# A new order for all engines in a state-space layer, half a product more on GpSimd, and the input image added earlier

## The chip, the cores and the metric

The kernel runs on one core of a Trainium2 chip. The metric is the device time of one execution in microseconds (us), as the median of the runs. The engines are TensorE (PE in the profile, PEld for its weight loads), VectorE (DVE), ScalarE (ACT), GpSimd (POOL) and the DMA queues, of which SyncE (SP) feeds the one used for plain transfers and GpSimd the one used for scatters.

## The reference, cut to what matters

Two layers on 32 images of 128 channels and 56 x 56 pixels, in float32. Layer 0 is a convolution with a mixture of experts, layer 1 a convolution with a selective scan (Mamba). With `L = 56 * 56` the tokens of an image and `DI = 256`, `DS = 16`:

```python
# layer 0: conv, LayerNorm, top 2 of 8 experts with capacity, then
return input + x_skip + layer_scale * moe_out
# layer 1, per image, t runs over the 3136 tokens
dt = softplus(dt @ dt_proj_w.T + dt_proj_b)
dA = exp(dt[..., None] * A)                      # 16 decays for each of 256 rows
dBu = dt[..., None] * Bm[:, :, None, :] * xm[..., None]
h = dA_t * h + dBu_t                             # the scan
y = einsum('bds,bs->bd', h, C_t) + xm * D
y = (y * silu(z)) @ out_proj_w.T
```

What is added at the end of layer 0 (`input + x_skip + moe_out`) is what layer 1 reads.

## The kernel before

The work runs in four stages, one after the other.

1. Layer 0's convolution, LayerNorm and routing. The normed rows go to `res_d` in DRAM, one row of 128 floats per token, each half row of 56 pixels in reversed order.
2. Dispatch: 56 batches, each of which loads 14 x 128 rows (`xg0`, six buffers deep), copies them on ScalarE (`xg1`) and scatters both with 28 indirect DMAs of GpSimd (L859) into `buf_d`. Half way, the weights of layer 1 are prepared.
3. The experts: rows are loaded from `buf_d`, go through two matrix products, and are added to `res_d` by indirect DMAs of GpSimd (L911).
4. Layer 1. Each image is cut into 7 groups of 448 tokens, 224 groups in all. A group has 16 units, one for each state. The 256 rows lie on 128 partitions as two halves.

In layer 1 the order on all engines is written out: `PLAN` lists the steps of a group, `UNITS` those of each unit, each with a place counted in units; the list of all groups is sorted by place and recorded in that order, under `manual_schedule`. Each engine then works through its own list in order and waits for semaphores. The places are an order and not times.

For a group, `fetch` loads a piece `x1` of the image and the rows `yg` of `res_d`; `moe_pe` (L1026, L1028) adds them on PE, with a permutation that turns the rows round; `moe_act` copies the sum to SBUF. Then follow a 1x1 convolution (`cv1_pe`, `cv1_act` with its tile `xh`), the variance (`sq_act`, `var_pe`, `rstd_act`, and `rstd_dve` in three tiny steps, L1090, L1092, L1095, the last of which writes `r`), `bc_pe` and `te_dve`, the projections `z_pe` and `xm_pe`, SiLU between two loads of activation tables (L1152, L1175), `px_pe`, `dt_pe`, the softplus (`sp_*`; `sp_pe` sums it into `p_sp`), and `sp_act`, which writes `dt` (L1240). `du_pool` multiplies dt and xm on GpSimd (L1245). The small matmuls share two PSUM buffers, `mm`.

For a unit: `bc_load` brings broadcast rows of B (`bb`) and C (`cb`), two units at a time. `db_pool` multiplies du and B for two units at once on GpSimd (L1336). `exp_act` writes the decays of both halves into one of two PSUM tiles, `da0` or `da1`, by the unit's parity (L1354). `scan_dve` runs the scan on VectorE (L1373, whole; L1377, by halves). `cmul` multiplies the states by C (L1397). `carry_act` saves the last state for the next group (L1405), `sum_pe` adds the product to the sum in PSUM (L1286). At the end come `yz_dve`, `out_pe` and `out_act`. rstd's first two steps work in the first four columns of da0, which the decays don't use.

`MODE` has a letter for each unit. D: whole scan in place, product on VectorE. P: whole scan into a tile `hs`, product on GpSimd. Q: as P, with the scan in two halves. M: two half scans, the first product half on VectorE, the second on GpSimd. Before it is `DQDDQDPPDDDDPDDP`: ten products on VectorE, six on GpSimd. `hs` has two buffers.

Of the kernel before, what the change touches and what calls it, by code (L numbers as in the profile page):

```python
# [42 lines left out]
MODE = 'DQDDQDPPDDDDPDDP'  # L43
PRODS = 6
PLAN = (
    (-41.157, "fetch"),
    (-34.382, "moe_pe"),
    (-32.986, "moe_act"),
    (-28.346, "cv1_pe", "p_cvc", "cv1c"),
    (-27.384, "sq_act"),  # L50
    (-26.393, "cv1_pe", "p_cv1", "cv1t"),
    (-25.274, "cv1_act"),
    (-23.306, "var_pe"),
    (-23.291, "rstd_act"),
    (-23.185, "edges_act"),
    (-20.935, "rstd_dve", 0),
    (-20.876, "rstd_dve", 1),
    (-19.458, "rstd_dve", 2),
    (-19.126, "bc_pe"),
    (-18.367, "te_dve"),  # L60
    (-18.165, "te_act"),
    (-17.77, "z_pe", 0),
    (-16.927, "z_copy", 0),
    (-15.982, "z_pe", 1),
    (-15.86, "xm_pe", 0),
    (-15.811, "xm_pe", 1),
    (-14.784, "z_copy", 1),
    (-14.441, "z_silu"),
    (-14.388, "xm_act", 0),
    (-14.349, "xm_act", 1),  # L70
    (-13.504, "tables"),
    (-13.487, "px_pe"),
    (-11.507, "px_act"),
    (-11.215, "dt_pe", 0),
    (-10.684, "dt_pe", 1),
    (-10.326, "sp_abs", 0),
    (-9.043, "sp_abs", 1),
    (-8.458, "sp_exp"),
    (-7.656, "sp_one"),
    (-6.228, "sp_w"),  # L80
    (-5.252, "sp_pe", ("w", "e", "m")),
    (-5.135, "sp_ln"),
    (-5.019, "sp_pe", ("u",)),
    (-4.678, "lt_pe", range(0, 9)),
    (-4.117, "sp_act", 0),
    (-3.918, "sp_act", 1),
    (-3.032, "lt_act", 0),
    (-3.001, "du_pool"),
    (-2.343, "lt_act", 1),
    (2.033, "lt_silu"),  # L90
    (3.656, "dd_pe"),
    (18.599, "yz_dve", 0),
    (18.857, "yz_dve", 1),
    (23.328, "out_pe"),
    (25.003, "out_act"),
# [3 lines left out]
        (-5.892, "bc_load", "bb"),  # L99
        (-3.501, "bc_load", "cb"),  # L100
        (-2.818, "db_pool"),
        (-0.991, "exp_act"),
        (-0.076, "scan_dve"),
        (0.16, "cmul", 0),
        (1.245, "carry_act"),
        (3.662, "sum_pe"),
    ),
    (
        (-2.505, "db_pool"),
        (-0.83, "exp_act"),  # L110
        (-0.619, "scan_dve"),
        (1.229, "cmul", 0),
        (3.088, "carry_act"),
        (9.441, "sum_pe"),
    ),
    (
        (-11.504, "bc_load", "bb"),
        (-2.533, "bc_load", "cb"),
        (-2.288, "db_pool"),
        (-0.633, "exp_act"),  # L120
        (-0.074, "scan_dve"),
        (0.16, "cmul", 0),
        (1.407, "carry_act"),
        (3.828, "sum_pe"),
    ),
    (
        (-3.007, "db_pool"),
        (-1.559, "exp_act"),
        (-0.609, "scan_dve"),
        (-0.338, "carry_act"),  # L130
        (0.16, "cmul", 0),
        (2.009, "sum_pe"),
    ),
    (
        (-4.093, "bc_load", "bb"),
        (-3.639, "db_pool"),
        (-0.666, "bc_load", "cb"),
        (-0.482, "exp_act"),
        (0.865, "scan_dve"),
        (1.06, "cmul", 0),  # L140
        (1.786, "sum_pe"),
        (2.033, "carry_act"),
    ),
    (
        (-4.025, "db_pool"),
        (-1.052, "exp_act"),
        (-0.068, "scan_dve"),
        (0.16, "cmul", 0),
        (1.263, "carry_act"),
        (3.791, "sum_pe"),  # L150
    ),
    (
        (-5.791, "bc_load", "bb"),
        (-4.743, "db_pool"),
        (-2.416, "bc_load", "cb"),
        (-0.463, "exp_act"),
        (0.538, "scan_dve"),
        (0.678, "cmul", 0),
        (1.758, "carry_act"),
        (4.239, "sum_pe"),  # L160
    ),
    (
        (-5.64, "db_pool"),
        (-0.299, "exp_act"),
        (-0.211, "scan_dve"),
        (1.06, "cmul", 0),
        (5.047, "sum_pe"),
        (5.187, "carry_act"),
    ),
    (  # L170
        (-7.178, "bc_load", "bb"),
        (-4.153, "db_pool"),
        (-3.514, "bc_load", "cb"),
        (-1.218, "exp_act"),
        (-0.956, "scan_dve"),
        (0.16, "cmul", 0),
        (0.466, "carry_act"),
        (0.815, "sum_pe"),
    ),
    (  # L180
        (-4.714, "db_pool"),
        (-1.825, "exp_act"),
        (-0.406, "scan_dve"),
        (0.16, "cmul", 0),
        (0.742, "carry_act"),
        (1.653, "sum_pe"),
    ),
    (
        (-8.23, "bc_load", "bb"),
        (-5.573, "bc_load", "cb"),  # L190
        (-4.053, "db_pool"),
        (-1.1, "exp_act"),
        (-0.6, "scan_dve"),
        (0.16, "cmul", 0),
        (0.996, "carry_act"),
        (1.077, "sum_pe"),
    ),
    (
        (-3.777, "db_pool"),
        (-0.685, "exp_act"),  # L200
        (-0.409, "scan_dve"),
        (0.16, "cmul", 0),
        (1.104, "sum_pe"),
        (1.278, "carry_act"),
    ),
    (
        (-7.87, "bc_load", "bb"),
        (-4.884, "bc_load", "cb"),
        (-4.31, "db_pool"),
        (-0.985, "exp_act"),  # L210
        (-0.749, "scan_dve"),
        (1.06, "cmul", 0),
        (5.159, "sum_pe"),
        (5.275, "carry_act"),
    ),
    (
        (-4.947, "db_pool"),
        (-0.443, "exp_act"),
        (0.085, "scan_dve"),
        (0.16, "cmul", 0),  # L220
        (0.197, "sum_pe"),
        (0.205, "carry_act"),
    ),
    (
        (-19.062, "bc_load", "bb"),
        (-4.926, "db_pool"),
        (-2.209, "bc_load", "cb"),
        (-1.206, "exp_act"),
        (-0.658, "scan_dve"),
        (0.16, "cmul", 0),  # L230
        (0.202, "sum_pe"),
        (0.903, "carry_act"),
    ),
    (
        (-3.892, "db_pool"),
        (-0.158, "exp_act"),
        (0.91, "scan_dve"),
        (1.06, "cmul", 0),
        (2.205, "carry_act"),
        (2.818, "sum_pe"),  # L240
# [4 lines left out]
def tile_kernel(tc: tile.TileContext, a: dict, out: bass.AP):  # L245
# [14 lines left out]
    with (  # L260
# [6 lines left out]
        res_d = dram.tile([T, C], F32, name="res_d")  # L267

        ident = const.tile([128, 128], F32, name="ident")
        make_identity(nc, ident)  # L270
        mean_w = const.tile([128, 128], F32, name="mean_w")
# [403 lines left out]
        def weights(wp, wt, pw):  # L675
# [86 lines left out]
            nc.tensor.matmul(p[:, 0:1], lhsT=mean_w, rhs=cv1b, start=True, stop=True)  # L762
# [66 lines left out]
        def apart(i, group):  # L829
            inst = i.ins  # L830
            tc.declare_no_dep(inst, group=group, reason="the rows differ")
            tc.add_to_no_dep_group(group, inst)

        with (
            tc.tile_pool(name="w3t", bufs=1, reuse_waits="tile") as w3t,
            tc.tile_pool(name="p3t", bufs=2, space=PSUM) as p3t,
            tc.tile_pool(name="dispc", bufs=1, reuse_waits="tile") as dc,
            tc.tile_pool(name="disp", bufs=6, reuse_waits="tile") as dp,
        ):
            backs = []  # L840
            for k in range(2):
                bi = dc.tile([128, QB, TT], I32, name=f"bi{k}")
                nc.gpsimd.iota(bi, pattern=[[TT, QB], [1, TT]], base=0, channel_multiplier=PT)
                backs.append(bi)
# [621 lines left out]
```

## Time and profile before

| what | value |
|---|---|
| median of 10 runs | 15843.36 us (15840.01 to 15850.96) |
| the profiled execution | 15844.33 us, its span 15842.5 us |
| mean granted clock of TensorE | 0.913 |
| busy: PE, DVE, ACT, POOL | 81%, 70%, 66%, 84% of the span |
| scatters of the dispatch (L859) | 1568, mean 1051 ns, 1767.9 to 3933.1 us |
| first and last `yg` load of layer 1 | 5878.4 and 15677.2 us |

The shares of the span are means over stages with different limits; a stage is read from a stretch of its own. A row of a group of instructions gives the line, engine, operation, tiles, shapes and count, then the total busy time and the mean duration in ns, then the idle time just before them and what ended it. A row of the order in time gives start, duration, engine, line and operation. Matmuls are pipelined and their ends are modelled, so a busy PE isn't PE at its peak.

### The profile page before, as it was taken

How to read it: one execution, taken by the hardware profiler on the slowest of the kernel's cores; microseconds unless marked ns; L12 is line 12 of the kernel's file. 1: busy time of each engine (PE TensorE's matmuls, PEld its weight loads, DVE VectorE, ACT ScalarE, POOL GpSimd, SP SyncE). 2: the span in 40 equal slices, each digit the busy share in tenths (PEclk: the TensorE clock that was granted, in tenths of full speed). 3: DMA queues.
4: the chain of work that ended last, by engine and by line, in shares of the span. 5: the costliest groups of instructions: out<-in, count | busy, mean ns of one | idle time of the engine just before them, and what ended most of it. 6: DMA issues, size and time to landing. Idle time of an engine off the chain costs nothing. (4 is left out here: it accounts for less than half of the span.)

```text
span 15842.5 us, 247520 instructions
## 1 busy us (share of the span) xinstructions
PE 12825.1 (81%) x92981; PEld 7167.8 (45%) x92981; DVE 11118.5 (70%) x11366; ACT 10517.5 (66%) x21038; POOL 13335.3 (84%) x6330
## 2 busy tenths in 40 slices
PE   7996200000999999999999999999999999999998
PEld 7996100000777764444444444444444444444444
DVE  2655400000111119999999999999999999999999
ACT  4565200000444448888888888888888888888888
POOL 2443477777888879999999999999999999999999
PEclk9997555555999999999999999999999999999999
DMA  8785422222555545555555555555555555555555
GB/s 268 230 238 175 169 72 71 71 71 65 68 72 70 72 64 184 185 184 185 185 184 185 184 185 184 185 185 184 183 183 184 185 184 183 185 183 184 183 183 171
DMA packets 1325280, 2520.85 MB, mean 159 GB/s; under 512 B 139352, under 2 KB 777136, under 8 KB 1316400
## 3 DMA queue, kind: packets, MB, share of 16 engines
q1 hardware_dynamic: 1127600, 2310.57, 45.4%
q0 software_dynamic: 196480, 194.45, 7.0%
q8 instruction: 732, 11.99, 0.3%
q14 instruction: 468, 3.83, 0.1%
HBM read 2129.06 MB, written 375.43 MB: 158 GB/s over the span
## 5 line engine op out<-in xcount | busy, mean ns | idle before, releaser
L1336 POOL TENSOR_TENSOR db<-du,bb 128x1792 f32<-128x1792 f32 x1792 | 6582.9, 3685 | 0.1
L1354 ACT ACTIVATE da<-dt,aneg 128x449 f32<-128x449 f32 x7168 | 4550.1, 639 | 372.7 <-DVE r L1095 112.0
L1373 DVE TENSOR_TENSOR_SCAN da<-da,db 128x898 f32<-128x898 f32 x2240 | 4524.3, 2020 | 0.6 <-issue 0.5
L1286 PE MATMUL py<-prod,ident 64*64 64x448 f32 x28672 | 3223.5, 547 | 117.6 <-DVE prod L1397 111.1
L1397 POOL TENSOR_TENSOR prod<-hs,cb 128x896 f32<-128x896 f32 x1344 | 2608.4, 1941 | 217.9 <-issue 157.1
L1397 DVE TENSOR_TENSOR prod<-da,cb 128x896 f32<-128x896 f32 x2240 | 2440.1, 1089 | 133.4 <-DMA cb<-bc_d 14.9
L859 POOL DMA_INDIRECT buf_d<-xg,slot x1568 | 1647.4, 1051 | 522.6 <-issue 518.3
L911 POOL DMA_INDIRECT res_d<-ys,xb x984 | 1591.8, 1618 | 350.8 <-issue 281.9
L951 PE MATMUL ept<-ident,xb 128*128 128x128 f32 (+1 forms) x984 | 189.0, 274 | 2078.9 <-DMA xb<-buf_d 2078.6
L1373 DVE TENSOR_TENSOR_SCAN hs<-da,db 128x898 f32<-128x898 f32 x896 | 1786.1, 2014 | 0.1
L1286 PEld LDWEIGHTS py<-prod,ident 64*64 64x64 f32 x28672 | 1008.8, 132 | 1554.4 <-issue 1102.1
L1126 PE MATMUL p_xm<-te,wk 128*128 128x448 f32 x3584 | 1395.4, 540 | 0.0
L903 DVE TENSOR_TENSOR ys<-py,b2t 128x512 f32<-128x512 f32 (+2 forms) x256 | 170.9, 670 | 1728.9 <-PE py L897 1602.7
L856 DVE COPY xg<-gate 128x14 f32<-128x14 f32 x112 | 20.6, 188 | 1884.8 <-DMA buf_d<-xg,slot 1830.5
L854 ACT COPY xg<-xg 128x1792 f32<-128x1792 f32 x56 | 94.6, 1690 | 1822.1 <-DMA buf_d<-xg,slot 1773.9
L951 PEld LDWEIGHTS ept<-ident,xb 128*128 128x128 f32 (+1 forms) x984 | 124.5, 143 | 2082.6 <-issue 2081.9
L897 PEld LDWEIGHTS py<-w2t,hh 128*128 128x128 f32 x7872 | 938.6, 192 | 191.2 <-issue 118.7
L897 PE MATMUL py<-w2t,hh 128*128 128x128 f32 x7872 | 988.1, 279 | 14.4 <-ACT hh L893 8.9
L1126 PEld LDWEIGHTS p_xm<-te,wk 128*128 128x128 f32 x3584 | 671.5, 189 | 665.4 <-issue 567.6
L379 PE MATMUL pc<-xc,toep 112*112 112x112 f32 (+1 forms) x8192 | 940.7, 271 | 35.7 <-ACT toep L368 31.9
L1377 DVE TENSOR_TENSOR_SCAN hs<-da,db 128x449 f32<-128x449 f32 x896 | 925.8, 1076 | 1.2 <-ACT db L1405 0.7
L1258 PE MATMUL p_l<-xh,dwd 64*64 64x224 f32 x16128 | 907.4, 352 | 22.4 <-ACT dt L1240 2.0
(241 smaller groups left out, 20299.4 us busy)
## 6 DMA issues: line engine op xcount, KB each, us to landing
bb<-bc_d SPq DMA_DIRECT2D x1792, 448.0 KB
cb<-bc_d SPq DMA_DIRECT2D x1792, 448.0 KB
toep<-toep_d SPq DMA_DIRECT2D x448, 392.0 KB
buf_d<-zero SPq DMA_DIRECT2D x28, 2275.0 KB
xb<-buf_d SPq DMA_DIRECT2D x240, 260.0 KB
xt<-in_x SPq DMA_DIRECT2D x32, 1568.0 KB
res_d<-xa SPq DMA_DIRECT2D x128, 392.0 KB
xg<-res_d SPq DMA_DIRECT2D x56, 896.0 KB
```

Source lines behind the costliest of these rows:

```text
L379: nc.tensor.matmul(pc[:, c, :, lo:hi], lhsT=tp[c // 2][:, c % 2, 6 - 2 * o : 8 - 2 * o, :], rhs=s4[:, c, :, lo + o - 1 : hi + o - 1], star ...
L859: apart(nc.gpsimd.indirect_dma_start(out=buf_d[:, :], out_offset=bass.IndirectOffsetOnAxis(ap=slots[k][:, o + j : o + j + 1], axis=0), in_ ...
L897: nc.tensor.matmul(py[:n, j, :], lhsT=hh[:, k, j * 128 : j * 128 + n], rhs=w2t[:, k, :], start=k == 0, stop=k == KF - 1,)
L911: apart(nc.gpsimd.indirect_dma_start(out=res_d[:, :], out_offset=bass.IndirectOffsetOnAxis(ap=xb[:n, j, C + 1 : C + 2].bitcast(I32), axis= ...
L1126: nc.tensor.matmul(p[:, :CH1], lhsT=s["wk"][:, k, hs], rhs=d["te"][:, k : k + CH1], start=k == 0, stop=k == DC - 1 and not first,)
L1258: nc.tensor.matmul(d["p_l"][r][k * HD : (k + 1) * HD, : CH1 // 2], lhsT=s["dwd"][rs, t, rs], rhs=d["xh"][rs, dy + k * R : dy + (k + 1) * R ...
L1286: nc.tensor.matmul(ps[r][h * HD : (h + 1) * HD, :CH1], lhsT=lhsT(rs, h), rhs=rhs[rs, h, :], start=start, stop=stop,)
L1336: nc.gpsimd.tensor_tensor(dbp[i // 2].rearrange("p k (h t) -> p k h t", h=2)[:, :, :, 1:], st[g]["du"].unsqueeze(1).to_broadcast(both), un ...
L1354: e = nc.scalar.activation(da[:, h * W1 : (h + 1) * W1], st[g]["dt"][:, h, :], AF.Exp, scale=s["aneg"][:, h, i : i + 1])
L1373: scans.append(nc.vector.tensor_tensor_scan(hs, da, dbs[i], 0.0, ALU.mult, ALU.add))
L1377: scans.append(nc.vector.tensor_tensor_scan(hs2[h][:, hh], da[:, hh], dbs[i][:, hh], 0.0, ALU.mult, ALU.add))
L1397: eng.tensor_tensor(w["prod"], w["hs"][0][:, :, 1:], w["cb"], ALU.mult)
```

## The change

The image's piece is no longer added in layer 1. In the dispatch a new function `skip` takes 64 parts (half an image each): it loads the image's part and the rows of `res_d`, turns the rows round and adds the image on PE, copies the sums on ScalarE, and stores them to a new `sum_d`. The experts' results are added to `sum_d`, with row numbers that count in natural order (`iota`). In layer 1 `fetch` loads only `yg`, and `moe_pe` is four plain transposes.

In layer 1 all places in `PLAN` and `UNITS` are new, the exps and the scans have a place for each half, and the modes are `PPDDMDPPDDPDPDDD`: nine whole products and a half on VectorE, six and a half on GpSimd. `hs` has three buffers, `x1` four. Orderings between steps that touch other bytes of one tile are taken out in a new way (`free`, `decay`). `final` picks the unit whose sum stands last.

The places of the steps that matter here, in units, of one group, before and after:

| step | before | after |
|---|---|---|
| rstd steps 1, 2 (group + 2) | 11.07, 11.12, ahead of product 11 | 9.59, 9.59, ahead of product 9 |
| exps of the next unit in da0 | unit 12: 11.02 | unit 10: 10.21, 10.28 |
| first table load to second (group + 1) | 1.56 to 2.50 | 2.76 to 3.74 |
| dt of the next group, then du | 11.88, 13.00 | 12.25, 14.16 |
| VectorE's order at the start | scan 0, product 0, scan 1, scan 2, product 2 | scans 0, 1, 2, 3, product 2 |

```diff
-MODE = 'DQDDQDPPDDDDPDDP'
+MODE = 'PPDDMDPPDDPDPDDD'
...
+            def skip(n, h):
+                t0 = (n * TPI + h * HT) * TT
+                xt = sk.tile([C, HT * TT], F32, name="xs")
+                nc.sync.dma_start(out=xt, in_=x_d[n, :, h * HT * TT : (h + 1) * HT * TT])
+                xr = sk.tile([TT, HT, C], F32, name="xr")
+                rows = [v[t0 : t0 + HT * TT, :].rearrange("(k p) c -> p k c", p=TT) for v in (res_d, sum_d)]
+                nc.sync.dma_start(out=xr, in_=rows[0])
+                for j0 in range(0, HT, 4):
+                    w = min(4, HT - j0)
+                    p = psk.tile([TT, 4, C], F32, name="p_sk")
+                    nc.tensor.matmul(p[:, :w], lhsT=perm, rhs=xr[:, j0 : j0 + w], start=True, stop=False)
+                    for j in range(w):
+                        nc.tensor.matmul(
+                            p[:, j, :], lhsT=xt[:, (j0 + j) * TT : (j0 + j + 1) * TT], rhs=ident,
+                            start=False, stop=j == w - 1,
+                        )
+                    nc.scalar.copy(xr[:, j0 : j0 + w], p[:, :w])
+                nc.sync.dma_start(out=rows[1], in_=xr)
...
+                    for _ in range(-(-len(parts) // (TT // XT * (QB - q) - p0 // XT))):
+                        skip(*parts.pop(0))
...
-                        out=res_d[:, :],
+                        out=sum_d[:, :],
...
-            nc.tensor.matmul(p[:, :CH1], lhsT=ident, rhs=d["x1"], start=True, stop=False)
             for j in range(TPC1):
-                nc.tensor.matmul(
-                    p[:, j * TT : (j + 1) * TT], lhsT=yg[:, j, :], rhs=perm, start=False, stop=j == TPC1 - 1
-                )
+                nc.tensor.transpose(p[:, j * TT : (j + 1) * TT], yg[:, j, :], ident[:TT, :TT])
...
+            away = mode in "PQ" or (mode == "M" and h == 1)
+            w.setdefault("hs", [da, da])
+            if away and (h == 0 or mode == "M"):
+                hs = three.tile([128, 2 * W1], F32, name="hs", bufs=3)
+                w["hs"] = [da, hs] if mode == "M" else [hs, hs]
```

## The prediction, on record before the result

> **What bounds the kernel now.** I read the stretches of the span first, then the groups of instructions, then the order in time of VectorE, ScalarE and GpSimd around one group of layer 1. The columns of the stretches are: length, busy time (instructions) of PE, PEld, DVE, ACT, POOL, granted clock, DMA share, GB/s.
>
> ```profile
> 2000.00:2500.00 500.00, 0.00 (x0) 0.00 (x0) 6.98 (x52) 21.97 (x13) 378.76 (x360) 0.50 0.24 72
> ...
> 8000.00:10000.00 2000.00, 1916.14 (x14118) 899.65 (x14117) 1972.38 (x1540) 1741.99 (x3606) 1923.06 (x692) 1.00 0.56 184
> ```
>
> The first line is the dispatch: only POOL works, 1568 scatters from 1767.9 to about 3935 us, 1.38 us each. The second is layer 1, two thirds of the span. The `r` step of L1095 starts at 6495.47 and, 194 groups later, at 15070.67: 44.20 us a group, 224 groups. VectorE is busy 98.6%, GpSimd 96.2%, PE 95.8% (modelled ends), ScalarE 87.1%.
>
> ```profile
> 10024.75 2.03 DVE L1373 TENSOR_TENSOR_SCAN da<-da,db 128x898 f32<-128x898 f32 x1
> 10026.68 0.15 DVE L1090 SCALAR_TENSOR_TENSOR da<-da,r 112x4 f32<-112x4 f32 x1
> 10026.86 0.17 DVE L1092 TENSOR_TENSOR da<-da,v 112x4 f32<-112x4 f32 x1
> 10026.94 1.08 DVE L1397 TENSOR_TENSOR prod<-da,cb 128x896 f32<-128x896 f32 x1
> 10027.94 2.02 DVE L1373 TENSOR_TENSOR_SCAN hs<-da,db 128x898 f32<-128x898 f32 x1
> 10029.87 0.14 DVE L1095 SCALAR_TENSOR_TENSOR r<-da,r 112x4 f32<-112x4 f32 x1
> 10029.93 2.03 DVE L1373 TENSOR_TENSOR_SCAN da<-da,db 128x898 f32<-128x898 f32 x1
> 10032.05 1.09 DVE L1397 TENSOR_TENSOR prod<-da,cb 128x896 f32<-128x896 f32 x1
> ```
>
> The reader is to see starts, not durations: after a scan an independent instruction starts 1.93 us later, a product of the same scan only after 2.04 to 2.13 us (mean 2.09, the last pair 2.12); a product holds the engine 1.00. One group by starts: 14 scans, 2 Q pairs (1.99), 10 products, two yz (1.18), te (0.52), the rstd steps (0.32) make 44.18, against 44.20 measured. So VectorE has no gap left to another engine: it is the bound, by its own list.
>
> ```profile
> L1336 POOL TENSOR_TENSOR db<-du,bb 128x1792 f32<-128x1792 f32 x1792 | 6582.9, 3685 | 0.1
> L1397 POOL TENSOR_TENSOR prod<-hs,cb 128x896 f32<-128x896 f32 x1344 | 2608.4, 1941 | 217.9 <-issue 157.1 <-DVE r L1095 18.4 <-DMA bb<-bc_d 16.8
> ...
> L1028 PE MATMUL p_moe<-perm,yg 112*128 112x112 f32 x1792 | 235.0, 274 | 23.4 <-DMA yg<-res_d 23.4
> ...
> L1026 PE MATMUL p_moe<-x,ident 128*128 128x448 f32 x448 | 228.9, 592 | 0.0
> ```
>
> GpSimd's idle time (some 2 us a group, before `prod` and `du`) is slack.
>
> **The change, part by part.** *VectorE, layer 1.* Ten whole products become nine and a half; two Q units (two half scans each) become one M and whole P scans. By starts, in the new order: 11 scans with something independent behind them, 11 x 1.93 = 21.23; only 5, 8 and 15 are followed at once by their own product, 3 x 2.09 = 6.27; scan 11 with the last rstd step, 2.10; M: its second half scan waits for the first (row 1.076, so 1.11), 0.99, and the half product 0.53 (nearest row: te and yz, 448 wide, 0.52 between starts); products 9 x 1.005 = 9.05; yz 1.18, te 0.52, rstd 0.26. Sum 43.24, 0.94 less than before: about half from the half product, half from products no longer right behind their scans.
>
> *What is late next.* I followed ScalarE's new order against this list. Three places cost VectorE time.
> First: in the plan before, the exps of unit 12 stand ahead of the first rstd step; now those of unit 10 stand behind it. They write da0, in whose first columns rstd works, so they wait for the second rstd step (L1092). VectorE has only product 9 between: 1.00 - 0.09 = 0.91 us from the end of the second rstd step, while two exps take 1.31 and the two signals 0.04 and 0.05, 1.40 in all. Stall 0.49.
> Second, the two table loads:
>
> ```profile
> 10041.81 2.55 ACT L1354 ACTIVATE da<-dt,aneg 128x449 f32<-128x449 f32 x4
> 10044.37 1.28 ACT L1152 ACT_TABLE_LOAD   x1
> 10045.67 0.95 ACT L1152 ACTIVATE zs<-zs 128x896 f32<-128x896 f32 x1
> 10046.52 1.14 ACT L1166 ACTIVATE xm<-p_xm,c1b 128x448 f32<-128x448 f32 x2
> 10047.56 0.58 ACT L1172 ACTIVATE lt<-lt 128x448 f32<-128x448 f32 x1
> 10048.15 1.28 ACT L1175 ACT_TABLE_LOAD   x1
> 10049.44 0.23 ACT L1405 COPY db<-da 128x2 f32<-128x2 f32 x2
> ```
>
> From load to next work this block is 5.07 us; now one carry copy (0.10) stands inside it. From the end of scan 1: 0.04, exps of unit 3 1.25, block 5.17, first exp of unit 4 0.64, signal 0.05 = 7.15. VectorE has 1.93 + 1.93 + 1.00 + 1.18 + 1.00 less 0.09 = 6.95 of work there. Stall 0.20.
> Third: exps of unit 11 stand behind unit 10's late ones, xh and two carries; 0.08. Elsewhere the cover is one scan (1.93) over two exps (1.40), or more. Period 43.24 + 0.77 = 44.0.
>
> *GpSimd.* Eight db, six products, du: 96.2% of 44.20 = 42.5. The half product lies on the line through 3.685 (1792 columns) and 1.941 (896): 1.07, between starts 1.03; bounds 0.97 and 1.94. So 43.5 (to 44.4), still under 44.0, but its slack falls from 1.7 to 0.5 us. The loop du, product 12, db0, db4, db2, scan 2 has 0.2 us of air (db 3.65 between starts; cover: scans 12 to 15). The third hs buffer spares scans a wait that the trace does not show (0.1 us before the hs scans): nothing.
>
> *PE.* The x matmuls of p_moe go (228.9 / 224 = 1.02 us) and two passes of 274 ns become one transpose (the expert stage's 128x128 transpose is one instruction of 273): 0.52. PE falls from 42.4 to 40.8 a group; it is not the bound, so this brings only air. The x1 load (224 KB a group) leaves the SP queue; bb and cb land 3 to 4 us after issue and in the new order are asked for 4 us or more ahead, the bb of unit 0 (behind the db of 14) with 1.5 us to spare: nothing.
> Layer 1: 223 periods x (44.0 - 44.2) = -45 us. Bounds: all stalls covered and GpSimd at 43.5, -156; stalls doubled, 44.8, +134.
>
> *Dispatch.* 64 parts: 2.4 MB of DMA each, four ScalarE copies of 0.65 (rows of 112 to 128 x 512), some 12.4 us of matmul at full clock (rows 274 and 0.66 for 512 columns), 25 if all run at half (p_sum there ranges from 492 to 1022 ns). 64 x 25 = 1600 us beside 2167 us of scatters: covered. On SP the part's store waits for ScalarE with the next xg load queued behind; xg is six deep, so five batches of 28 x 1.38 = 193 us cover that. Are the scatters slowed by the extra 71 GB/s? Around an xg load (2040 to 2042 us, DMA share 1.12) they keep starting every 1.27 us. Low end 0; high end: every 20 to 40 us some issue is slow, in all (1.38 - 1.27) x 1568 = 175 us, which could double. I take +5, near the low end, because the expert stage at share 0.52 has no more such idle time (281.9 us over 984).
> [...]
> [...]
>
> *Ends.* The last unit's product is now VectorE's (1.09 for 1.94): -1. The run-in keeps its chain: 0.
> Sum on the profiled execution (15844.3 us, span 15842.5, 1.0 above the median): 15844.3 - 45 + 5 - 1 = 15803; for the median 15802, 0.26% less.
>
> **Rivals.** *A, the stalls are covered:* if the rstd wait costs nothing, GpSimd's 43.5 plus 0.1 sets the pace: -0.6 x 223 = -134, 15713. For it: the order before showed no stall at all. Against it: 1.31 us of exps behind 0.91 us of product.
> *B, slower: the dt chain.* GpSimd, short of slack, waits in du for dt, dt for p_sp, and p_sp for both PSUM buffers of mm, the last freed by xh, which now stands behind the late exps. If dt comes over 0.2 us later than in my list, db2 is late and scan 2 stalls by the rest. Before, du already waits 0.6 to 1.2 us here, off the path. At 0.8 us late the period is 44.6: 223 x 0.4 = +89, plus 5: 15936. It decides from 0.4 us late, where the gain is gone.
> *C, nothing:* 44.2 again, stalls eating the whole 0.94: 15848.
>
> **How the numbers follow.** Forecast 0.45, A 0.22, B 0.23, C 0.10. A measurement can tell about 0.2%, 32 us, from no change. The forecast, 0.15 us either way (33 us), lies beyond 0.2% in about three fifths of its cases: 0.29; with A and a little of C, faster 0.52. Slower: B and a little of C, 0.25. Same: 0.23. Range for 8 in 10: from 15690 (A with GpSimd at 43.5) to 15935 (B).
>
> **What would show it.** Right: r of L1095's counterpart every 44.0 us; VectorE idle before the hs scan of unit 10, released by ScalarE da, near 0.5 us a group; GpSimd near 99%; dispatch still 2165 to 2180 us. Wrong: VectorE idle before scan 2 released by GpSimd db (B), a period under 43.7 (A), or scatters more than 1.42 us apart.

## The result, and the profile after

The changed kernel takes 15930.4 us (median; runs from 15909.6 to 15991.3) beside 15843.8 us of the kernel before (15837.3 to 15851.7): a ratio of 1.0060, 95% interval 1.0051 to 1.0068. It is slower by 0.6%, where 0.26% faster was forecast. Its runs are spread over 82 us where those of before are spread over 14. The profiled execution took 15978.7 us, with a span of 15977.0.

By stages (first and last starts of the scatters and of the yg loads in the two traces):

| stage | before | after | difference |
|---|---|---|---|
| up to the first scatter of the dispatch | 1767.9 | 1776.8 | +8.9 |
| scatters of the dispatch, first to last | 2165.2 | 2341.8 | +176.6 |
| from there to the first scatter of the expert stage | 37.7 | 19.4 | -18.3 |
| scatters of the expert stage | 1904.6 | 1900.6 | -4.0 |
| first yg load to the end (layer 1) | 9964.2 | 9935.3 | -28.9 |

The first difference is not the change's: another profile of the kernel before has its first scatter at 1775.7. So layer 1 gained 29 us and the dispatch lost 177, of which it gave 18 back at its end.

The two stretches shown of before, now of the changed kernel (length, busy time and instructions of PE, PEld, DVE, ACT, POOL, granted clock, DMA share, GB/s):

```profile
2000.00:2500.00 500.00, 91.78 (x366) 62.55 (x366) 10.87 (x59) 40.91 (x57) 306.16 (x320) 0.56 0.39 113
8000.00:10000.00 2000.00, 1900.51 (x13894) 871.06 (x13893) 1952.85 (x1500) 1736.76 (x3663) 1969.13 (x741) 1.00 0.55 179
```

In the first, GpSimd issues 320 scatters where it issued 360. In the second, GpSimd has risen to 98.5% and VectorE has fallen to 97.6%. VectorE's order in time around the rstd steps (start, duration, instruction; in brackets the idle time before it and what ended it):

```profile
10041.01 2.03 DVE L1416 TENSOR_TENSOR_SCAN da<-da,db 128x898 f32<-128x898 f32 x1
10042.94 0.15 DVE L1141 SCALAR_TENSOR_TENSOR da<-da,r 112x4 f32<-112x4 f32 x1
10043.12 0.17 DVE L1143 TENSOR_TENSOR da<-da,v 112x4 f32<-112x4 f32 x1
10043.20 1.08 DVE L1429 TENSOR_TENSOR prod<-da,cb 128x896 f32<-128x896 f32 x1
10044.67 2.03 DVE L1416 TENSOR_TENSOR_SCAN hs<-da,db 128x898 f32<-128x898 f32 x1 [0.39 <-ACT da L1400]
```

This is the wait that was forecast: the hs scan of unit 10 waits for ScalarE's exps, which stand behind the second rstd step. What went wrong is in what GpSimd waited for in the dispatch (waits of GpSimd from 1770 to 4130 us: total, times, longest):

```profile
POOL buf_d L899 <- issue: 465.4, 1523, 1.3
...
POOL buf_d L899 <- DMA xg<-res_d: 199.5, 14, 25.5
POOL buf_d L899 <- ACT xg L894: 150.1, 15, 19.4
POOL buf_d L899 <- ACT xr L883: 25.8, 3, 12.7
```

The first line is the 0.30 us between two scatters. The others, 375 us, are new: xg was not there, either its load or ScalarE's copy of it. Against them stands a gain: when not waiting, the scatters now start every 1.26 us and not every 1.38, some 180 us in all, because the long ones are almost gone. The scatters of before and after (duration in ns min/median/max, first and last start):

```profile
L859 POOL DMA_INDIRECT buf_d<-xg,slot x1568: 966/971/1930, 1767.9 to 3933.1; - x196
L899 POOL DMA_INDIRECT buf_d<-xg,slot x1568: 952/958/1221, 1776.8 to 4118.6; - x196
```

Why was xg late? Three engines at one place, each in the order of time. First TensorE, then ScalarE:

```profile
1858.43 2.02 PE L877 MATMUL p_sk<-xr,perm 112*112 112x512 f32 x2 [63.37 <-issue]
1860.24 1.92 PE L879 MATMUL p_sk<-ident,xs 128*112 128x128 f32 x8
1861.95 1.49 PE L877 MATMUL p_sk<-xr,perm 112*112 112x512 f32 x2
1863.27 1.04 PE L879 MATMUL p_sk<-ident,xs 128*112 128x128 f32 x8
```

```profile
1876.79 0.58 ACT L883 COPY xr<-p_sk 112x512 f32<-112x512 f32 x1 [26.09 <-remote]
1904.77 0.58 ACT L883 COPY xr<-p_sk 112x512 f32<-112x512 f32 x1 [27.39 <-remote]
1932.07 0.58 ACT L883 COPY xr<-p_sk 112x512 f32<-112x512 f32 x1 [26.71 <-remote]
1932.55 1.69 ACT L894 COPY xg<-xg 128x1792 f32<-128x1792 f32 x1
1948.87 0.37 ACT L883 COPY xr<-p_sk 112x256 f32<-112x256 f32 x1 [14.63 <-remote]
1976.91 0.58 ACT L883 COPY xr<-p_sk 112x512 f32<-112x512 f32 x1 [27.67 <-remote]
```

A block of a part is one product with perm (2 instructions and 2 weight loads in the trace) and four of the image (8 and 8): 20 TensorE instructions, 12 in the short block that ends each part. By their records the first two blocks are done at 1862 and 1864 us. But ScalarE's copies of them start at 1876.8 and 1904.8, and the second waited for TensorE's semaphore alone; the page can only say "remote", because no TensorE instruction is recorded as ending there. The copies of whole blocks come 28.0, 27.3 and 28.0 us apart, that of a short block 16.8: 1.40 us for each TensorE instruction (20 x 1.40 = 28.0, 12 x 1.40 = 16.8). In that stretch the copy of xg at 1932.55 stands behind such a copy in ScalarE's order, and SyncE's order shows the rest:

```profile
1854.48 9.66 SPq L893 DMA_DIRECT2D xg<-res_d  x2
1948.86 0.35 SPq L870 DMA_DIRECT2D xs<-in_x  x1
1949.32 0.37 SPq L884 DMA_DIRECT2D sum_d<-xr  x1
1955.12 0.71 SPq L893 DMA_DIRECT2D xg<-res_d  x1
```

From 1864 to 1949 us SyncE issues nothing. First in its queue stands the load of an image part (L870), which waits for TensorE to be done with the buffer (the page again names "remote"), then the store of a part's sums (L884), which waits for ScalarE's copies, and the next xg load is queued behind both. Over the dispatch SyncE waits 821 us for ScalarE before L884, and 419 us before L870 with "remote" as the cause.

### The profile page after: what moved, and what is told of

It is laid out like the page before. It is cut to its first block, busy times and chain, and to the rows that moved or that the text cites. A ratio compares the mean times of both kernels' runs of the same rounds, so it can differ in the third digit from the quotient of the medians.

```text
span 15977.0 us, 249108 instructions
## 1 busy us (share of the span) xinstructions
PE 13345.8 (84%) x93941; PEld 7441.6 (47%) x93941; DVE 10992.2 (69%) x11143; ACT 10576.5 (66%) x21486; POOL 13388.2 (84%) x6554
## 3 DMA queue, kind: packets, MB, share of 16 engines
q1 hardware_dynamic: 1307312, 2413.33, 47.9%
## 5 line engine op out<-in xcount | busy, mean ns | idle before, releaser
L1416 DVE TENSOR_TENSOR_SCAN da<-da,db 128x898 f32<-128x898 f32 (+1 forms) x2240 | 4275.2, 1927 | 54.8 <-ACT da L1400 52.4
L1416 DVE TENSOR_TENSOR_SCAN hs<-da,db 128x898 f32<-128x898 f32 (+1 forms) x1568 | 2915.0, 1883 | 112.1 <-ACT da L1400 88.3
L1429 POOL TENSOR_TENSOR prod<-hs,cb 128x896 f32<-128x896 f32 x1344 | 2583.6, 1937 | 48.6 <-issue 13.5
L1429 DVE TENSOR_TENSOR prod<-da,cb 128x896 f32<-128x896 f32 x2016 | 2188.3, 1086 | 42.3 <-DMA cb<-bc_d 6.1
L899 POOL DMA_INDIRECT buf_d<-xg,slot x1568 | 1501.6, 958 | 844.9 <-issue 465.4
L953 POOL DMA_INDIRECT sum_d<-ys,xb x984 | 1589.2, 1615 | 331.3 <-issue 285.3
L877 PE MATMUL p_sk<-xr,perm 112*112 112x512 f32 (+1 forms) x512 | 358.7, 793 | 1608.0 <-issue 976.0
L883 ACT COPY xr<-p_sk 112x512 f32<-112x512 f32 (+1 forms) x256 | 132.3, 533 | 1977.9 <-remote 1395.6
L390 PEld LDWEIGHTS pc<-xc,toep 112*112 112x112 f32 x8192 | 884.6, 185 | 47.2 <-ACT toep L379 41.0
L420 POOL TENSOR_TENSOR xa<-xa,lng 112x896 f32<-112x896 f32 x128 | 267.3, 2088 | 747.4 <-ACT xa L417 688.1
L932 PE MATMUL ph<-xc,w1t 128*128 128x512 f32 (+1 forms) x1984 | 885.1, 589 | 0.0
```

Of the source, the lines that this page charges most:

```text
L390: nc.tensor.matmul(pc[:, c, :, lo:hi], lhsT=tp[c // 2][:, c % 2, 6 - 2 * o : 8 - 2 * o, :], rhs=s4[:, c, :, lo + o - 1 : hi + o - 1], star ...
L877: nc.tensor.matmul(p[:, :w], lhsT=perm, rhs=xr[:, j0 : j0 + w], start=True, stop=False)
L899: apart(nc.gpsimd.indirect_dma_start(out=buf_d[:, :], out_offset=bass.IndirectOffsetOnAxis(ap=slots[k][:, o + j : o + j + 1], axis=0), in_ ...
L932: nc.tensor.matmul(ph[:, :rows], lhsT=w1t[:, k * 128 : (k + 1) * 128], rhs=xc[:, :rows], start=True, stop=True)
L953: apart(nc.gpsimd.indirect_dma_start(out=sum_d[:, :], out_offset=bass.IndirectOffsetOnAxis(ap=xb[:n, j, C + 1 : C + 2].bitcast(I32), axis= ...
L1416: scan = nc.vector.tensor_tensor_scan(w["hs"][h][:, hh], da[:, hh], dbs[i][:, hh], 0.0, ALU.mult, ALU.add)
```

## The experiments

Runs that are compared shared a chip. Four chips took part, and they turned out to be of two kinds: beside the first four experiments the kernel before took 15846 us, beside the next four 15653, beside the rest 15849 and 15844. Whether the chip itself makes the difference, or what runs around it, was not tested. Ratios are to the kernel before on the same chip.

Two theories at the start. L: TensorE's reports of finished blocks come late while the scatters run, and in two in-order engines everything for the scatters is queued behind them. D: the 150 MB of the parts hold up loads or scatters. Beside these, Q: the order in SyncE's queue alone.

**e1_skip_only**: the diff's dispatch part put into the kernel before, which keeps its own order in layer 1 and reads sum_d there by transposes.

> The kernel before with the dispatch part of the change alone (image added to rows between the scatters; layer 1 reads the sums, in the order of before). Theory L (TensorE reports its sums late while scatters run, 28 us for a block of ten matmul pairs; ScalarE's copies wait for that, and behind them in ScalarE's and SyncE's order stand the copies and loads of xg): the scatters take 2300 to 2380 us instead of 2165, the first yg load comes about 163 us later than in before, layer 1 keeps its 44.20 us, and the time is 15843 + 163 = 16006, spread over some 80 us from run to run. If the loss of the changed kernel sits in layer 1's new order and not in the dispatch, this one is within 30 us of 15843.

Measured 16003.9 us, ratio 1.0099 (1.0082 to 1.0116). The scatters take 2305.7 us, as expected. Layer 1 takes 10001.8 us from the first yg load, 37.6 more than before, where no difference was expected. Half of its groups still take 44.14 us or less, but of the 200 groups in the middle 48 take over 44.5, where 15 of before did; why was not tested.

**e2_order_only**: the other half.

```diff
-                    for _ in range(-(-len(parts) // (TT // XT * (QB - q) - p0 // XT))):
-                        skip(*parts.pop(0))
...
-                        out=sum_d[:, :],
+                        out=res_d[:, :],
...
+    (-37.5, "fetch_x"),
     (-32.6293, "moe_pe"),
...
+            nc.tensor.matmul(p[:, :CH1], lhsT=ident, rhs=d["x1"], start=True, stop=False)
             for j in range(TPC1):
-                nc.tensor.transpose(p[:, j * TT : (j + 1) * TT], yg[:, j, :], ident[:TT, :TT])
+                nc.tensor.matmul(
+                    p[:, j * TT : (j + 1) * TT], lhsT=yg[:, j, :], rhs=perm, start=False, stop=j == TPC1 - 1
+                )
```

> The changed kernel without the dispatch part: layer 1 in its new order, but the image is loaded and added there by TensorE as before (its load is a step of its own at place -37.5, so that four input buffers are enough). If the new order brings by itself what the trace of the changed kernel shows (44.08 us a group in place of 44.20): dispatch 2165, time 15843 - 28 = 15815. If TensorE's three or four passes more a group, or the load of 224 KB, cost something in the new order, the period goes back to 44.2 and the time to 15843 or above.

Measured 15908.1 us, ratio 1.0040 (1.0026 to 1.0054). The dispatch is back at 2165.0 us, but layer 1 takes 10023.3, 59 more than before, with single groups of 44.4 us. VectorE's two largest waits from 7000 to 15000 us in this kernel:

```profile
DVE yz L1312 <- PE py L1322: 131.4, 180, 1.3
DVE hs L1396 <- ACT da L1380: 71.0, 182, 0.5
```

The first is 13.5 us in the changed kernel: with the image's passes on TensorE again, the sums that yz needs come 0.7 us late in every group. So in layer 1 each half of the change alone loses (37.6 and 59 us) and both together gain 29.

**e3_moves_only**: the parts keep their loads and their store; products and copies go.

```diff
-                for j0 in range(0, HT, 4):
-                    ...
-                    nc.scalar.copy(xr[:, j0 : j0 + w], p[:, :w])
```

> The changed kernel with TensorE's products and ScalarE's copies of the 64 parts left out: both loads and the store of a part stay, on the same queue and in the same order, so the image is not added. Theory L: nothing late is left to wait for, the xg loads come in time, scatters 2165 to 2190 us, time 15815 to 15840. Rival D (the 150 MB themselves hold up the xg loads or the scatters): scatters still 2300 or more, time about 15930.

Measured 15816.2 us, ratio 0.9981 (0.9971 to 0.9990). The line of the scatters (duration min/median/max, first and last start):

```profile
L889 POOL DMA_INDIRECT buf_d<-xg,slot x1568: 954/958/2075, 1767.8 to 3934.0; - x196
```

2166.2 us: the 150 MB cost nothing, on the same queue and in the same order. D falls, and so does Q in its plain form: the stores ahead of the xg loads do no harm when nothing makes them late.

**e4_skip_apart**: the parts' DMAs on ScalarE's queue, and xg copied by VectorE.

```diff
-                nc.sync.dma_start(out=xt, in_=x_d[n, :, h * HT * TT : (h + 1) * HT * TT])
+                nc.scalar.dma_start(out=xt, in_=x_d[n, :, h * HT * TT : (h + 1) * HT * TT])
...
-                nc.sync.dma_start(out=xr, in_=rows[0])
+                nc.scalar.dma_start(out=xr, in_=rows[0])
...
-                nc.sync.dma_start(out=rows[1], in_=xr)
+                nc.scalar.dma_start(out=rows[1], in_=xr)
...
-                    nc.scalar.copy(xgs[1][:, :, :C], xgs[0][:, :, :C])
+                    nc.vector.tensor_copy(xgs[1][:, :, :C], xgs[0][:, :, :C])
```

> The changed kernel with the loads and the store of a part issued by ScalarE, and the copy of xg made by VectorE: nothing that the scatters need stands behind a part any more. Theory L: GpSimd no longer waits for xg and the scatters take 2165 to 2200 us; but then nothing interrupts the scatters and TensorE stays late, so some parts end after the last scatter, and the expert stage's sums wait for them: 28 us for each block of ten pairs would be 6451 us in all if no block came quickly, so the time lies anywhere above 15815, and the trace tells how far. Rival Q (only the order in SyncE's queue matters, TensorE is quick enough by itself): scatters 2165 to 2190, all parts done with them, time 15815.

Measured 16031.2 us, ratio 1.0121 (1.0104 to 1.0138), scatters over 2349.5 us. Neither theory's number for the scatters came out: GpSimd still waits for xg. What SyncE and GpSimd waited for in this dispatch:

```profile
SPq L893 <- DMA xr<-res_d: 544.0, 9, 161.2
SPq L893 <- DMA sum_d<-xr: 535.3, 8, 96.6
```

```profile
POOL buf_d L899 <- DMA xg<-res_d: 338.7, 15, 35.6
```

So an xg load still stood behind a part's DMA (1079 us in these two rows), though no longer in its queue. In the changed kernel's trace SyncE's 5599 DMAs land on eight semaphores in turn; whether the two queues of e4 share such a set, and wait for each other by it, is not shown. The edit did not take the parts apart from xg, and decides nothing between L and Q.

The next four were meant for the lateness itself.

**e5_perm_only**: the four image products of each block left out.

> The changed kernel with the four products of the image left out of every block (a block keeps the one product with perm: 4 TensorE instructions, loads counted, in place of 20), so the image is not added; loads, copies, stores, queues and waits stay. Theory I (under the scatters each TensorE instruction takes 1.40 us: 28.0 us between the reports of blocks of 20 instructions, 16.8 between those of 12): 5.6 us a block, 256 x 5.6 = 1434 us, less than the 2165 of the scatters; scatters 2165 to 2200 us, time 15816 to 15850. Theory B (a late report for each block, whatever it holds): 28 us a block again, scatters about 2340, time about 15930.

**e6_ahead**: all calls of skip ahead of the loop over xg. The kernel that ran kept all five products of a block (20 instructions); the text on record is wrong there.

> The changed kernel with blocks of the product with perm alone, as in the run before this one, and all 64 parts ahead of the first scatter. What is asked is how soon TensorE's reports come without scatters beside them: theory of both kinds, within 4 us of the product, and the parts go at the pace of their 150 MB, 600 to 800 us at 190 to 250 GB/s; scatters afterwards 2165; time 16420 to 16620. If the lateness has nothing to do with the scatters, the reports stay 5.6 us or more apart here too, and the parts take 1434 us or more.

**e7_aside**: `aside = one.tile([TT, TPC1], F32, name="aside")` in place of `das[0][:TT, :TPC1]`.

> The changed kernel with the rstd steps' values in a tile of their own, not in the first columns of the tile that the exps of unit 10 write. Theory S (VectorE waits 0.39 us a group for those exps, and they for the second rstd step, for the sake of that tile alone): that wait goes, the period falls from 44.0 to 43.6 (GpSimd, 98.5% busy, allows 43.4), 0.4 x 223 = 89 us: about 15841. Rival P (the pace is GpSimd's or TensorE's, the wait only fills air): period 44.0 again, 15930.

**e8_fewer**: 12 instructions a block.

```diff
+                    pt = psk.tile([TT, 4, C], F32, name="p_xt")
                     for j in range(w):
-                        nc.tensor.matmul(
-                            p[:, j, :], lhsT=xt[:, (j0 + j) * TT : (j0 + j + 1) * TT], rhs=ident,
-                            start=False, stop=j == w - 1,
-                        )
+                        nc.tensor.transpose(pt[:, j, :], xt[:, (j0 + j) * TT : (j0 + j + 1) * TT], ident)
                     nc.scalar.copy(xr[:, j0 : j0 + w], p[:, :w])
+                    nc.vector.tensor_tensor(xr[:, j0 : j0 + w], xr[:, j0 : j0 + w], pt[:, :w], ALU.add)
```

> The changed kernel with 12 TensorE instructions a block in place of 20: the image's tiles are transposed in one pass into a tile of their own, ScalarE copies the product with perm, and VectorE adds. Theory I: 16.8 us a block in place of 28.0 (11.2 for 16.8 in the short ones), 3942 us in all in place of 6093 were nothing quick, so the waits of GpSimd shrink by about a third of their 370 us or more: scatters 2200 to 2260 us, time 15850 to 15890. Theory B: 2340 us and 15930 again. VectorE's adds stand ahead of its copies into xg, which could cost a few us where ScalarE's copies did.

Measured beside 15653.1 us of before: e5 15611.0 (0.9973, 0.9962 to 0.9984), e6 15625.0 (one run), e7 16491.1 (1.0536), e8 15614.3 (0.9976, 0.9967 to 0.9985). On this chip the question about TensorE could not be asked, because nothing was late. The scatters' line in e8, and ScalarE's copies in e7, whose blocks are the changed kernel's:

```profile
L898 POOL DMA_INDIRECT buf_d<-xg,slot x1568: 954/958/1980, 1765.4 to 3746.5; - x196
```

```profile
2099.95 0.59 ACT L883 COPY xr<-p_sk 112x512 f32<-112x512 f32 x1 [1.15 <-PE p_sk L879]
2100.82 0.37 ACT L883 COPY xr<-p_sk 112x256 f32<-112x256 f32 x1 [0.28 <-PE p_sk L879]
```

In all four the scatters take 1979 to 1981 us (1.262 us each), whatever the blocks hold, and the copies follow the products. In e6 the scatters began at 1783.7 and the parts went beside them, not ahead, so its own question stayed unanswered. So these runs show the change without its loss in the dispatch: e5 and e8 0.24 to 0.27% less than before, e6, which keeps the blocks of the changed kernel, 0.18% less.

e7 did the opposite of both theories: VectorE's wait before hs is gone, but a group takes 47.9 us. Two groups of its lines from 7000 to 15000 us (busy us, mean ns | idle before):

```profile
L1143 DVE TENSOR_TENSOR aside<-aside,v 112x4 f32<-112x4 f32 x167 | 466.4, 2793 | 5.7
L1141 DVE SCALAR_TENSOR_TENSOR aside<-aside,r 112x4 f32<-112x4 f32 x167 | 287.3, 1720 | 0.0
```

The same steps on 112 x 4 values take 171 and 146 ns with one operand in PSUM (0.17 and 0.15 us in the timeline above). With both in SBUF L1143 takes 2.62 us more in the mean; one starts at 10028.76 and takes 3.60 us. Why is not shown: the third step, L1146, takes 249 ns with both its operands in SBUF. So in this kernel the tile is better off in PSUM, and e7 says nothing on what the wait costs.

**before_here and after_again**, unchanged kernels, and **e9_other_bank**, the wait taken away another way: the exp of unit 10's second half, which writes the other half of the tile da0 (the other bank in the words of its expectation), no longer waits for rstd.

```diff
-            return free(i, (b, h), [(b, 1 - h)] if h < 2 else [])
+            return free(i, (b, h), ([(b, 1 - h)] if h < 2 else []) + (["aside"] if (b, h) == (0, 1) else []))
+
+        def rstd(i):
+            return free(i, "aside", [(0, 1)])
...
-                nc.vector.tensor_tensor(aside, aside, d.pop("v"), ALU.mult)
+                rstd(nc.vector.tensor_tensor(aside, aside, d.pop("v"), ALU.mult))
```

**e10_fewer_bank** is e8 and e9 together.

> The kernel before, for its trace. The last four runs had a kernel before of 15653 us beside them where the first four had 15846, and in their traces all scatters of the dispatch start 1.262 us apart (1979 us in all). Theory M (the dispatch differs by machine: where the scatters' writes lag, GpSimd waits for room and TensorE's reports come late; where they do not, neither happens): the kernel before shows either 1979 us of scatters and 15653 us, or 2165 us and 15844 us, and the changed kernel beside it loses time in the dispatch in the second case only. Rival: 2165 us here whatever the time, and the kernels tried last were quick for what they left out.

> The changed kernel once more. Theory M: if the kernel before takes about 15653 us here, the scatters take 1979 us, TensorE's reports come with their products, and the time is that of before less what layer 1 gains, 28 us, and a few us of the expert stage: 15620, or 0.998; if before takes about 15845, the scatters take 2300 or more and the ratio is 1.005 again. Rival: 1.005 on either.

> The changed kernel in which the exp of the second half of unit 10, which lies in another PSUM bank than the rstd steps' values, no longer waits for them; the first half's still does. Theory S: only one exp of 0.64 us is then left behind the second rstd step, 0.64 + 0.09 of signals under the 0.91 us that product 9 gives, so VectorE's wait of 0.39 us before the hs scan of unit 10 goes, the period falls from 44.0 to 43.6, GpSimd allowing 43.4, and the time by 0.4 x 223 = 89 us against the changed kernel of this call. Rival P (the pace is set by GpSimd's or TensorE's own list): VectorE waits elsewhere, and the period stays at 43.9 to 44.0.

> The blocks of 12 TensorE instructions and the exp without its wait together. Theories M and S: 89 us less than the changed kernel where the scatters do not lag, so 0.992 of before; where they lag, the changed kernel's loss in the dispatch shrinks by a third or more too: 0.997 of before or less. Rival P: 0.998 and 1.001 to 1.002.

Beside 15849.3 us of before: before_here 15845.0 with scatters over 2165.4 us; after_again 15950.0, 1.0061 (1.0048 to 1.0075), scatters 2330.9; e9 15818.2, 0.9979 (0.9970 to 0.9988); e10 15786.9, 0.9959 (0.9946 to 0.9973), scatters 2252.1. This is M's second case; that GpSimd waits for room there, as M has it, no row shows. VectorE in e9, in place of the lines shown above, and one stretch:

```profile
10033.84 0.17 DVE L1147 TENSOR_TENSOR da<-da,v 112x4 f32<-112x4 f32 x1
10033.92 1.08 DVE L1433 TENSOR_TENSOR prod<-da,cb 128x896 f32<-128x896 f32 x1
10034.92 2.02 DVE L1420 TENSOR_TENSOR_SCAN hs<-da,db 128x898 f32<-128x898 f32 x1
```

```profile
8000.00:10000.00 2000.00, 1925.38 (x14095) 882.13 (x14094) 1971.63 (x1518) 1756.16 (x3701) 1992.43 (x750) 1.00 0.57 182
```

The hs scan follows its product in 1.00 us with no wait. Single groups take 43.46 us in place of 44.00, and GpSimd is busy 99.6%: it is the bound now. Theory S holds; from the first r to the last, 9691.7 us in place of 9808.9 in after_again, 117 less.

**e11_no_scatters, after_third, e12_both_again**: the changed kernel without the 1568 scatters, as it is, and e10's kernel again.

> The changed kernel with the 1568 scatters of the dispatch left out; all parts, loads, copies and stores stay, so the experts get rows of zeros. Theory I (the scatters make TensorE's reports late): every report comes with its product, the parts go at the pace of their DMAs, 64 x 2.4 MB and 56 x 0.9 MB at some 200 GB/s, 700 to 1000 us, and the time is 15930 less 1300 to 1600. Rival T (TensorE's reports are late on that machine whenever it works in short bursts): lags of 20 us and more here too.

> The changed kernel a third time. Theory M: where the kernel before takes about 15653 us, 1979 us of scatters, no lag of TensorE, and 15615 to 15625 us; where it takes about 15845, scatters of 2300 us or more and a ratio of 1.005 to 1.007 again.

> Blocks of 12 instructions and the exp without its wait, once more. Theory M: where the kernel before takes about 15653 us, 15614 less 117 = 15497, a ratio of 0.990; where it takes about 15845, 0.996 again.

Beside 15844.5 us of before: e11 14395.4 (one run); after_third 15965.0, 1.0076 (1.0055 to 1.0097), scatters 2302.0, copies of whole blocks again 28.0 us apart; e12 15774.5, 0.9953 (0.9936 to 0.9969), scatters 2272.3. ScalarE in e11:

```profile
1907.34 0.58 ACT L883 COPY xr<-p_sk 112x512 f32<-112x512 f32 x1 [6.98 <-PE p_sk L879]
1909.03 0.58 ACT L883 COPY xr<-p_sk 112x512 f32<-112x512 f32 x1 [1.11 <-PE p_sk L879]
1910.76 0.58 ACT L883 COPY xr<-p_sk 112x512 f32<-112x512 f32 x1 [1.15 <-PE p_sk L879]
```

On the chip on which the changed kernel lost, with the same blocks of 20 instructions, the copies come 1.7 us apart once the scatters are gone; all 64 parts are stored by 2545.7 us, 784 after the first xr load. So the scatters make the reports late (theory I, against T). And in e12, with blocks of 12:

```profile
2146.39 0.59 ACT L881 COPY xr<-p_sk 112x512 f32<-112x512 f32 x1 [10.14 <-remote]
...
2162.49 0.59 ACT L881 COPY xr<-p_sk 112x512 f32<-112x512 f32 x1 [13.93 <-remote]
2179.28 0.59 ACT L881 COPY xr<-p_sk 112x512 f32<-112x512 f32 x1 [16.21 <-issue]
...
2196.79 0.37 ACT L881 COPY xr<-p_sk 112x256 f32<-112x256 f32 x1 [15.33 <-remote]
```

16.1, 16.8 and 17.5 us: 12 x 1.40 = 16.8. These copies wait only for the first product of their block, so that 12 instructions lie between two of them ahead of the short block too. VectorE's adds wait for a whole block, 12 instructions or, in the short one, 8:

```profile
2173.06 0.69 DVE L882 TENSOR_TENSOR xr<-xr,p_xt 112x512 f32<-112x512 f32 x1 [15.94 <-issue]
2189.86 0.69 DVE L882 TENSOR_TENSOR xr<-xr,p_xt 112x512 f32<-112x512 f32 x1 [16.11 <-remote]
...
2201.06 0.42 DVE L882 TENSOR_TENSOR xr<-xr,p_xt 112x256 f32<-112x256 f32 x1 [10.34 <-remote]
```

16.8 and 11.2 us, 12 and 8 times 1.40. The price is per instruction, not per report, and fewer instructions shorten GpSimd's waits of over 2 us: 363 us in after_again, 275 in e10; 325 in after_third, 294 in e12. Theory I expected the loss to shrink by a third or more. Over the 2165 us of before, the scatters lose 87 us in e10 for 166 in after_again, about half, but 107 in e12 for 137 in after_third, about a fifth.

## Why the prediction was wrong

*The dispatch: the step that failed.* "64 x 25 = 1600 us beside 2167 us of scatters: covered", and "xg is six deep, so five batches cover that". The rows from which 25 us a part came are rows of stages without these scatters. Beside them a part takes 3 x 28.0 + 16.8 = 100.8 us by the spacing of ScalarE's copies, 64 parts 6451: three times the stage. Nothing covers that, and a buffer six deep only delays the loss, because the copy of xg and the load of xg are in order behind the parts on both engines that feed it. The parts progress in good part while GpSimd, out of xg, pauses: 93 of ScalarE's 256 copies start in its 29 pauses of over 2 us, 371 us of the 2342. In e11, with no scatter, the parts need 784 us in all. The forecast +5 was 177, and the scatters came 1.49 us apart in the mean, over the 1.42 that the prediction names as a sign of being wrong. That its upper bound (175 us) came near is chance: it priced slower scatters, which e3 shows not to exist (2166.2 us with all DMAs).

*What it could not have known from one trace.* The scatters of before were 1.38 us apart with slow issues among them, 1.262 on the one chip where no block was late. There the forecast dispatch is what e5, e7 and e8 show (no wait of GpSimd over 2 us). That the ratios of e5 and e8, 0.9973 and 0.9976, are the forecast one (0.9974) is partly chance: they are 42 and 39 us less than before, but their layer 1, from the first r to the last, is only 31 and 28 us shorter than the 9842.0 of before, where 45 were forecast; where the rest comes from is not shown. The changed kernel itself was not timed on such a chip.

*Layer 1: right in kind, smaller.* Predicted 44.20 to 44.0, -45 us. The 44.20 was a mean over 194 groups with some slow ones among them, where most groups of before take 44.15; the 44.0 was a sum for one group without such. Most groups do take 44.01 now, but every seventh takes 44.26 in the mean, and the mean over the same 194 groups is 44.07. So 0.13 us a group was gained and not 0.20, and the 223 periods give 9842.0 to 9813.0: -29. Of the stalls, 0.49 was 0.39 (hs of unit 10), 0.20 was 0.26 (scan 4a, in 155 groups of 182), the third, 0.08, is not to be seen. M's second half starts 1.20 us after the first (forecast 1.11), and its product takes 600 ns. GpSimd's 98.5% is the forecast "near 99%", its half product 982 ns for 1.07 us.

*TensorE's relief "brings only air": wrong.* e2 shows that the new order needs that air: without it single groups take 44.4 us and yz waits for TensorE. TensorE's busy time fell from 42.4 to 41.9 us a group, where 40.8 was forecast; why by less is not shown.

*The rivals.* B did not happen: du waits for dt 0.5 us at most, 4 us in 8000. A's condition was false in the changed kernel, but its price was about right: with the rstd wait taken away e9's groups take 43.46 us, for the 43.6 put there. C is out. No rival had the loss in the dispatch, the one place where the change put new work into three in-order queues at once; the slower case was sought in layer 1 alone. The measured 15930 us lies just inside the stated range, to 15935, but that end was B's sum; the loss came from elsewhere, so this is luck.

*Left open.* Why scatters make TensorE's reports cost 1.40 us an instruction, and why on three chips of four. The lateness could also be the recording's. No run here separates that; the times of the changed kernel's other executions (15909.6 to 15991.3) lie on both sides of the profiled one's (15978.7), and whether those were free of records is not known. What the two traces of before and after do show is that the recording itself has gaps: 126 of the 10287 instructions of TensorE that update its semaphore lack their update in the changed kernel, 140 of 9805 in the kernel before, all of them between the first and the last of GpSimd's indirect DMAs, none ahead of them or in layer 1. This fits the recording as a cause and does not show it: 84 of the 126 are missing in the expert stage, and there ScalarE's longest wait for TensorE is 3.9 us and VectorE's 6.8.

## What to carry to other kernels

Durations of an engine's instructions are worth no more than the stage from which they are taken (here 25 us a part by rows of other stages, 100.8 beside the scatters): before work is called covered, ask what else runs in the stage and whether any row shows the two together; if none does, the bound is open upwards. Count the in-order queues through which the bottleneck is fed, and keep new work that waits for a third engine out of all of them; a deep buffer does not help when both its load and its copy are queued behind that wait (xg is six deep here, and GpSimd waited 375 us for it). When two halves of a change are measured apart, do not trust their sum: here each alone cost layer 1 time and both together saved it, and the mended version (12 instructions a block, one exp freed from a wait) beats both kernels, at 0.9953 to 0.9959 of before where the changed kernel took 1.0061 to 1.0076.

## What the runs showed of the hardware

- While the scatters of the dispatch ran back to back, on three chips of four, the engines that waited for TensorE saw its blocks end 1.40 us per instruction apart, weight loads counted, whatever their size (112x512 or 128x128): 28.0 us for 20, 16.8 for 12, 11.2 for 8. The recorded times of the matmuls show none of it. Without the scatters it did not occur (copies 1.7 us apart in e11), nor beside the expert stage's scatters, where ScalarE's 711 waits for the first of TensorE's two products (L932) come to 154 us, 2.9 at the longest.
- The same kernel before took 15653 us on one chip and 15844 to 15849 on three; in the kernels traced there the dispatch scatters took 1979 to 1981 us, against 2165 of the kernel before on two of the others.
- VectorE's second rstd step (L1143, 112 x 4 values) took 2793 ns in e7 with both operands in SBUF, 171 ns in the changed kernel with one in PSUM.
- In e4 the xg loads of SyncE waited 1079 us for DMAs of the parts that ScalarE had issued (544.0 for xr, 535.3 for sum_d).
